# The norm of the sampled image channel by channel in one operation, and the last tap's copy on VectorE

## The chip, the cores and the metric

The kernel runs on one core of one Trainium2 chip. The metric is the device time of one execution in microseconds, as the median of several runs; lower is better. Before the change the three runs gave 17384.59, 17384.90 and 17401.33 us, median 17384.9.

## The reference, cut to what matters

A network of four layers works on `x` of shape (16, 32, 128, 128) in float32: 16 images, 32 channels, 128 x 128 pixels. Each layer adds its result to its input. The change lies in the last part of layer 1, a deformable convolution along a row of nine taps: each tap samples the normalised input at a row position that differs from pixel to pixel, then the nine samples are combined by a convolution, and a group norm over groups of four channels follows.

```python
K = 9
y = weight * yk + y_new
y_map = y.transpose(0, 2, 1, 3).reshape(Bn, Wd * K, Hd)
...
deformed = grid_sample_bilinear(input, grid)
out = conv2d(deformed, dsc_w, dsc_b, stride=(K, 1))
return group_norm(out, gn_w, gn_b, gn_w.shape[0] // 4)

# in the network
x = x + _L1_conv_ref(_gn(x), ...)
```

Before this part, other functions have made the sampling positions `y` for every tap and pixel (`ymap` in the kernel). A tap's column is a whole number, its row is not, so bilinear sampling is a weighted sum over rows, with the hat function max(0, 1 - |row - y|) as weight.

## The kernel before

The program runs through the layers one after the other. `layer1_sample` is the stage of the change. For each of the 16 images it holds the input as a tile `xt` of 128 rows (partitions) by 32 channels by 128 columns, and goes through 32 blocks of four columns. `order` lists all 512 (image, block) pairs; the loop variable `m` counts them, `n` is the block within its image, and `s, i = divmod(n, 4)` splits it into a group `s` of four blocks and the block's place `i` in the group.

**Sampling as a matmul.** For a tap the weights of all 128 rows are laid out as a hat matrix: row number against pixel. The kernel spreads the positions over all partitions, either with a DMA that broadcasts them (tile `yd`, taps 4 to 7, function `fetch`) or with matmuls by a selection matrix into PSUM tile `pb` (`spread`, tile `ya` for taps 0 to 3, tile `h8` for the ninth tap of a whole group of four blocks). ScalarE takes |y - row| of them (L1236 for `yd`, L1116 for `ya` and `h8`), VectorE makes min(., 1) - 1, the negative hat (`hats`, L1120). TensorE then multiplies `xt` by the hats (`sample`, L1127), 32 small matmuls per call, into a PSUM tile `pd` of 128 x 512; the pool of `pd` has two buffers. VectorE copies each `pd` to SBUF tile `ds` (L1274 for taps 0 to 3, L1280 for taps 4 to 7).

**The ninth tap.** Once a group, at `i == 3`, `last_tap` samples with `h8` into a `pd`, and that is copied to SBUF tile `ds8` (L1301), by ScalarE in this version. Straight after it VectorE makes the hats of the next group's `h8`.

**The convolution and the finish.** At `i == 0` of the next group `convolve` multiplies the group's samples by the weights (L1162, L1167) into PSUM tile `po`, and ScalarE adds the bias and copies (L1170). At `i == 1` `turn` transposes the result and VectorE copies it into the image's result tile `ob` (L1180), 128 partitions by 32 channels by 128. When an image's last group has been turned, `finish` starts for it. It is a Python generator: each `next(done)` at the end of a block of the next image issues its instructions up to the following `yield`. It has 22 such parts, so it spreads over blocks 1 to 22 of the next image: eight with the statistics of four channels each (L1193, L1194), two with small operations for mean and scale (two small matmuls by `avg`, L1197 and L1206), and twelve that apply the norm. The norm of four channels is a scale and an offset for each partition and channel, `sc` and `bi`, 128 x 8 x 4 each. The twelve parts are four slices `o` of eight channels with three operations of 128 x 1024 elements each: times `sc` (L1223), plus `bi` (L1225), both read by a broadcast along the 128 columns, and plus `xt` (L1227), after which GpSimd issues the DMA that stores the eight channels to `x2` (L1228). After the loop the rest of the last image's finish is issued at once.

**What sets the order.** TensorE, VectorE and ScalarE take their instructions in the order in which the program writes them, because the loop stands in `in_order`. GpSimd only stores the results here. The SP queue loads `yd` for every block (L1105), and per image `Y` and `Y8` (L1085, L1089) and `xt` in four pieces (L1093); their place on SP is chosen by the framework that schedules the program. `xt` has two buffers, so that its next load waits for the last L1227 of the image that used the buffer.

Of the kernel before, what the change touches and what calls it, by code (L numbers as in the profile page):

```python
# [12 lines left out]
ALU = mybir.AluOpType  # L13
# [4 lines left out]
P = 128  # L18
B, T, HW = 16, 32, 128
# [18 lines left out]
def rstd_of(nc, pool, var, n, m, tag):  # L38

    r = pool.tile([n, m], F32, name=tag, tag=tag)  # L40
    nc.vector.tensor_scalar_add(r, var, EPS)
    nc.scalar.activation(r, r, AF.Sqrt)
    nc.vector.reciprocal(r, r)
    return r


@contextmanager
def in_order(tc, *engines):

    traced = tc.nc.cur_bb.bb.instructions  # L50
    last = traced[-1]
    yield
    start = next(k for k in reversed(range(len(traced))) if traced[k] is last) + 1
    of = {e.engine: None for e in engines}
    for i in traced[start:]:
        if i.engine in of:
            if of[i.engine] is not None:
                tc.add_manual_dep(
                    i, of[i.engine].name,
                    mybir.DependencyInfo(mybir.DependencyClass.NoSync, mybir.DependencyReason.DATA),  # L60
                    reason="program order",
                )
            of[i.engine] = i
# [961 lines left out]
def layer1_sample(tc, w, x1, x2, ymap, sb1, batches=range(B)):  # L1025
# [9 lines left out]
    V, S, M = nc.vector, nc.scalar, nc.tensor.matmul  # L1035
# [3 lines left out]
    with ExitStack() as ctx:  # L1039
# [61 lines left out]
        def fetch(m):  # L1101
            b, n = order[m]
            blocks[m] = bl = {}
            bl["yd"] = yd = hp.tile([P, 4, W4], F32, name="yd", tag="yd", bufs=4)
            nc.sync.dma_start(  # L1105
                yd, ym(b)[4:8, n * W4 : n * W4 + W4].unsqueeze(0).to_broadcast([P, 4, W4])
            )
# [10 lines left out]
        def hats(t):  # L1118

            V.tensor_scalar(t, t, 1.0, 1.0, ALU.min, ALU.subtract)  # L1120
# [11 lines left out]
        def taps(m, k0, h):  # L1132
            b, n = order[m]
            pd = psd.tile([P, 4, HW], F32, name="pd", tag="pd")
            sample(
                pd, b,
                [
                    (q, i, 4 * n + i + k0 + q - 4, h[:, q, HW * i : HW * i + HW])
                    for i in range(4) for q in range(4)
                ],  # L1140
            )
            return pd
# [42 lines left out]
        def finish(b):  # L1185

            g, j = divmod(b, 4)
            im = images[b]
            ob, xt = im["ob"], im["xt"]
            st = sp.tile([P, 8, 6], F32, name="st", tag="st")  # L1190
            mv = sp.tile([P, 8, 2], F32, name="mv", tag="mv")
            for og in range(8):
                V.bn_stats(st[:, og], ob[:, 4 * og : 4 * og + 4])  # L1193
                V.bn_aggr(mv[:, og], st[:, og])  # L1194
                yield
            pm = pso.tile([P, 4, P], F32, name="pm", tag="pt")[:, 0, 0:8]
            M(pm, avg, mv[:, :, 0], start=True, stop=True)  # L1197
            mean = sp.tile([P, 8], F32, name="mean", tag="mean")
            V.tensor_copy(mean, pm)
            d = sp.tile([P, 8], F32, name="d", tag="d")  # L1200
            V.tensor_sub(d, mv[:, :, 0], mean)
            V.tensor_mul(d, d, d)
            V.tensor_add(d, d, mv[:, :, 1])
            yield
            pv = pso.tile([P, 4, P], F32, name="pv", tag="pt")[:, 0, 0:8]
            M(pv, avg, d, start=True, stop=True)  # L1206
            r = rstd_of(nc, sp, pv, P, 8, "r8")
            sc = sp.tile([P, 8, 4], F32, name="sc", tag="sc")
            V.tensor_mul(
                sc, rows[:, 0].rearrange("p (a b) -> p a b", b=4),  # L1210
                r.unsqueeze(2).to_broadcast([P, 8, 4]),
            )
            bi = sp.tile([P, 8, 4], F32, name="bi", tag="bi")
            V.tensor_mul(bi, sc, mean.unsqueeze(2).to_broadcast([P, 8, 4]))
            V.tensor_sub(bi, rows[:, 1].rearrange("p (a b) -> p a b", b=4), bi)
            yield
            for q in range(4):
                o = slice(8 * q, 8 * q + 8)
                col = [
                    t.rearrange("p a b -> p (a b)")[:, o].unsqueeze(2).to_broadcast([P, 8, HW])  # L1220
                    for t in (sc, bi)
                ]
                V.tensor_mul(ob[:, o], ob[:, o], col[0])  # L1223
                yield
                V.tensor_add(ob[:, o], ob[:, o], col[1])  # L1225
                yield
                V.tensor_add(ob[:, o], ob[:, o], xt[:, o])  # L1227
                nc.gpsimd.dma_start(  # L1228
                    x2[g][T * j + 8 * q : T * j + 8 * q + 8].rearrange("o (r c) -> r o c", c=HW),
                    ob[:, o],  # L1230
                )
                yield

        def absolutes(m):
            yd = blocks[m]["yd"]
            S.activation(yd, yd, AF.Abs, bias=nrow)  # L1236

        def near(m):
            b, n = order[m]
            blocks[m]["ya"] = ya = hp.tile([P, 4, W4], F32, name="ya", tag="ya")  # L1240
            spread(ya, images[b]["Y"], n, 32)

        def eighth(b, s):
            h8 = hp.tile([P, 4, W4], F32, name="h8", tag="h8", bufs=2)
            spread(h8, images[b]["Y8"], s, 8)
            images[b]["h8", s] = h8
# [5 lines left out]
        with in_order(tc, nc.tensor, nc.vector, nc.scalar):  # L1252
            eighth(batches[0], 0)
            near(0)
            absolutes(0)
            near(1)
            hats(images[batches[0]]["h8", 0])
            hats(blocks[0]["ya"])
            hats(blocks[0]["yd"])
            done = iter(())  # L1260
            for m in range(NM + 6):
                b, n = order[m] if m < NM else (None, m - NM)
                if m < NM:
                    bl = blocks[m]
                    bl["ds"] = dp.tile([P, 2, W4], F32, name="ds", tag="ds", bufs=6)
                    if n == 12 and m + NB < NM:
                        open_image(order[m + NB][0])
                    if m + 3 < NM:
                        fetch(m + 3)
                    pd = taps(m, 0, bl["ya"])  # L1270
                    if m + 1 < NM:
                        absolutes(m + 1)
                        hats(blocks[m + 1]["ya"])
                    V.tensor_copy(bl["ds"][:, 0], pd.rearrange("p i r -> p (i r)"))  # L1274
                    if m + 2 < NM:
                        near(m + 2)
                    pd = taps(m, 4, bl["yd"])
                    if m + 1 < NM:
                        hats(blocks[m + 1]["yd"])
                    V.tensor_copy(bl["ds"][:, 1], pd.rearrange("p i r -> p (i r)"))  # L1280
                s, i = divmod(n, 4)
                if i == 0 and 4 <= m <= NM:
                    bb, nn = order[m - 4]
                    ss = nn // 4
                    oc = convolve(
                        bb, ss, [blocks.pop(mm)["ds"] for mm in range(m - 4, m)],
                        images[bb].pop("ds8"),
                    )
                elif i == 1 and 5 <= m <= NM + 1:
                    turn(bb, ss, oc)  # L1290
                    if ss == NB // 4 - 1:
                        for _ in done:
                            pass
                        done = finish(bb)
                elif i == 2 and m + 2 < NM:
                    nb_, nn = order[m + 2]
                    eighth(nb_, nn // 4)
                elif i == 3 and m < NM:
                    pd = last_tap(b, s, images[b].pop(("h8", s)))
                    ds8 = dp.tile([P, W4], F32, name="ds8", tag="ds8")  # L1300
                    S.copy(ds8, pd.rearrange("p i r -> p (i r)"))  # L1301
                    images[b]["ds8"] = ds8
                    if m + 1 < NM:
                        nb_, nn = order[m + 1]
                        hats(images[nb_]["h8", nn // 4])
                next(done, None)
            for _ in done:
                pass
# [1033 lines left out]
```

## Time and profile before

The profiled execution took 17350.9 us, of which its span, from the first to the last instruction of the core, is 17349.1 us. The sampling stage lies between 11.17 and 14.36 ms of the span; ahead of it come layer 0 and the positions, behind it layers 2 and 3.

| | us |
|---|---|
| median of three runs | 17384.9 |
| profiled execution | 17350.9 |
| its span | 17349.1 |
| first load of positions into the stage to its last store | about 3190 |

The span's busy times by stretch (GpSimd is nearly idle in the sampling stage):

| stretch, ms | TensorE | VectorE | ScalarE | GpSimd | granted clock of TensorE |
|---|---|---|---|---|---|
| 0 to 5.7 | 5268 | 5380 | 4593 | 5628 | 0.99 |
| 6.5 to 11.9 | 4731 | 4992 | 3972 | 3786 | 0.94 |
| 11.9 to 17.35 | 4699 | 3891 | 3228 | 121 | 0.86 |

Within the sampling stage the start of the bias operation L1170, once per group of four blocks, is a clock tick. The mean interval between two of them, by the group's place in its image, is this (group 0 is blocks 1 to 4 in the image's numbering, group 1 is blocks 5 to 8, and so on, since L1170 runs in the first block of a group):

| group in the image | 0 | 1 | 2 | 3 | 4 | 5 | 6 | 7 |
|---|---|---|---|---|---|---|---|---|
| mean interval, us | 23.37 | 23.83 | 25.67 | 24.27 | 24.02 | 23.56 | 26.11 | 23.94 |
| parts of `finish` in it | 4 statistics | 4 statistics | mean, scale, 2 norm | 4 norm | 4 norm | 2 norm | none | none |

To read such tables: an engine's busy time counts every moment in which it has an instruction under way. On VectorE and ScalarE an instruction's own duration is longer than the distance to the next start, since the next begins before the last has drained; so a row's mean duration times its count overstates what an instruction takes of the engine. Distances between starts are named as such below.

### The profile page before, as it was taken

To read this page: it belongs to the slowest core of one execution; us is meant where nothing else is said; L and a number is where in the kernel's file an instruction comes from. 1 tells how busy PE (TensorE), PEld (TensorE's weight loads), DVE (VectorE), ACT (ScalarE), POOL (GpSimd) and SP (SyncE) were. 2 spreads that over 40 slices of the span, in tenths; PEclk is the share of its full clock that TensorE was granted. 3 is DMA by queue.
4 is the path that set the end of the run, shared out by engine and by line. 5 is a ranking of instruction groups with operands and counts; after the bars stand their busy time and mean duration, and the time that the engine had idled before them with its cause. 6 is when DMAs were issued, how large, how long until landed. Compare 5 with 4: busy or idle time off the path is not lost. (4 is left out here: it accounts for less than half of the span.)

```text
span 17349.1 us, 299637 instructions
## 1 busy us (share of the span) xinstructions
PE 15374.5 (89%) x113040; PEld 5889.8 (34%) x113040; DVE 14782.1 (85%) x14857; ACT 12219.8 (70%) x23708; POOL 9818.0 (57%) x18465
## 2 busy tenths in 40 slices
PE   8999999999999888888888888899999997688988
PEld 3333333333333322222222222255555552233433
DVE  9999999999999759999999999888888886777523
ACT  7888888888888647777777777698898882455311
POOL 9999999999999617778888888600000000000000
PEclk9999999999999989999999999898999888778888
DMA  0000000000000484444554445577777779444345
GB/s 22 12 12 12 12 12 16 12 12 12 12 13 10 70 146 155 164 161 156 166 163 163 164 161 167 158 187 198 198 196 194 198 196 206 89 77 79 72 117 177
DMA packets 1525970, 1884.46 MB, mean 109 GB/s; under 512 B 148837, under 2 KB 868765, under 8 KB 1513702
## 3 DMA queue, kind: packets, MB, share of 16 engines
q1 hardware_dynamic: 1413414, 1688.04, 37.6%
q10 hardware_dynamic: 84480, 83.91, 1.6%
q0 software_dynamic: 26624, 93.35, 1.5%
q8 instruction: 888, 14.55, 0.3%
q14 instruction: 564, 4.62, 0.1%
HBM read 1561.58 MB, written 229.64 MB: 103 GB/s over the span
## 5 line engine op out<-in xcount | busy, mean ns | idle before, releaser
L235 POOL TENSOR_SCALAR Rp<-su,nv 128x128 f32<-128x128 f32 x16384 | 5837.5, 378 | 71.7 <-PE pS L241 37.8
L224 DVE TENSOR_TENSOR Rd<-pu,nv 128x2048 f32<-128x2048 f32 x2176 | 4880.8, 2277 | 75.3 <-PE pS L241 71.6
L239 ACT ACTIVATE Ra<-su,bv 128x128 f32<-128x128 f32 x14336 | 4285.5, 388 | 540.9 <-PE pS L241 536.3
L241 PE MATMUL pS<-Rd,zw 128*32 128x512 f32 x17408 | 2907.3, 603 | 219.4 <-DVE Rd L224 219.1
L822 DVE TENSOR_TENSOR_SCAN hh<-dd,state,pd 128x512 f32<-128x512 f32 x2304 | 2823.0, 1267 | 153.7 <-PE py L856 10.6
L843 POOL TENSOR_TENSOR hh<-hh,bc 128x2048 f32<-128x2048 f32 x512 | 2319.8, 4531 | 458.4 <-DVE state L830 455.2
L241 PE MATMUL pS<-Rp,zw 128*32 128x512 f32 x8192 | 2012.3, 596 | 175.1 <-POOL Rp L235 173.2
L807 PE MATMUL pd<-du,spread 32*128 32x512 f32 x4608 | 1352.1, 661 | 571.0 <-DVE hh L822 563.1
L1228 POOL DMA_DIRECT2D x<-ob x64 | 89.4, 1396 | 3098.8 <-DVE ob L1227 2762.4
L799 ACT ACTIVATE dd<-dd,m_a 128x512 f32<-128x512 f32 x2304 | 1515.2, 714 | 339.0 <-DMA dd<-dm 328.2
L817 DVE TENSOR_TENSOR pd<-pd,bc 128x1024 f32<-128x1024 f32 x1152 | 1400.5, 1216 | 61.8 <-ACT bc L780 53.0
L241 PE MATMUL pS<-Ra,zw 128*32 128x512 f32 x7168 | 1276.2, 600 | 0.0
L1236 ACT ACTIVATE yd<-yd,nrow 128x2048 f32<-128x2048 f32 x512 | 1235.2, 2412 | 39.9 <-DMA yd<-ymap 39.9
L1116 ACT ACTIVATE ya<-pb,nrow 128x1024 f32<-128x1024 f32 x1024 | 1191.3, 1255 | 81.8 <-PE pb L1115 81.6
L1115 PE MATMUL pb<-Y,sel 32*128 32x512 f32 (+1 forms) x5120 | 1089.2, 744 | 160.6 <-ACT ya L1116 157.4
L241 PEld LDWEIGHTS pS<-Rd,zw 128*32 128x32 f32 x17408 | 623.7, 109 | 1225.2 <-issue 586.8
L807 PEld LDWEIGHTS pd<-du,spread 32*128 32x128 f32 x4608 | 373.7, 191 | 1611.6 <-DVE hh L822 717.7
L241 PEld LDWEIGHTS pS<-Rp,zw 128*32 128x32 f32 x8192 | 443.2, 109 | 1322.6 <-POOL Rp L235 863.3
L1120 DVE TENSOR_SCALAR yd<-yd 128x2048 f32<-128x2048 f32 x512 | 724.4, 1415 | 184.6 <-ACT yd L1236 183.4
L1120 DVE TENSOR_SCALAR ya<-ya 128x2048 f32<-128x2048 f32 x512 | 753.8, 1472 | 9.9 <-ACT ya L1116 8.8
L1127 PE MATMUL pd<-ya,xt 128*32 128x128 f32 x16384 | 688.7, 310 | 40.6 <-DVE ds L1280 29.6
L1127 PEld LDWEIGHTS pd<-yd,xt 128*32 128x32 f32 x16384 | 539.8, 178 | 470.2 <-issue 232.9
(421 smaller groups left out, 23716.8 us busy)
## 6 DMA issues: line engine op xcount, KB each, us to landing
dd<-dm SPq DMA_DIRECT2D x2304, 256.0 KB
yd<-ymap SPq DMA_DIRECT2D x512, 1024.0 KB
hw<-x SPq DMA_DIRECT2D x192, 512.0 KB
dm<-dt POOLq DMA_DIRECT2D x192, 256.0 KB, 3.9
xb<-tok SPq DMA_DIRECT2D x248, 144.0 KB
w<-d SPq DMA_DIRECT2D x64, 528.1 KB
x<-in_x SPq DMA_DIRECT2D x64, 512.0 KB
x<-o SPq DMA_DIRECT2D x128, 256.0 KB
```

What stands on the lines that cost most here:

```text
L224: nc.vector.tensor_tensor(R, st["pu"].unsqueeze(1).to_broadcast([P, 4, 4, HW]), nv[:, :, i::32].rearrange("p t q -> p q t").unsqueeze(3).t ...
L235: nc.gpsimd.tensor_scalar(R[:, q, k], su[:, k], 3.4028234e38, nv[:, k, c], ALU.min, ALU.max)
L239: nc.scalar.activation(R[:, q, k], su[:, k], AF.Relu, bias=bv[:, k, c])
L241: nc.tensor.matmul(st["pS"][32 * q : 32 * q + 32], zw[:, 31 - i : 63 - i], R[:, q], start=first, stop=False, tile_position=(0, 32 * q), sk ...
L799: S.activation(dd[:, r], dd[:, r], AF.Exp, scale=acol[:, dr, d : d + 1])
L807: nc.tensor.matmul(pd[:, a], spread[e, k], st["du"][n][e], start=True, stop=True)
L817: V.tensor_mul(pd, pd, bm.unsqueeze(1).to_broadcast([P, 2, CH]))
L822: V.tensor_tensor_scan(hh[:, r, s], dd[:, r, s], pd[:, a, s], st["state"][:, 4 * i + r : 4 * i + r + 1], ALU.mult, ALU.add,)
L843: G.tensor_mul(hh, hh, st["bc"][1, n].unsqueeze(1).to_broadcast([P, 4, CH]))
L1120: V.tensor_scalar(t, t, 1.0, 1.0, ALU.min, ALU.subtract)
L1127: M(pd[32 * q : 32 * q + 32, i], xt[:, :, xc], h, start=True, stop=True, tile_position=(0, 32 * q),)
L1236: S.activation(yd, yd, AF.Abs, bias=nrow)
```

## The change

Two edits, both in `layer1_sample`. In `finish`, the two operations over eight channels with broadcast scale and offset are replaced by eight operations of one channel each, which multiply and add in one instruction, with the scale and the offset of that channel as scalars per partition. There is a `yield` after every fourth channel, so a slice still takes two parts for these and one for the addition of `xt`. In the loop, the copy of the last tap's samples from PSUM to `ds8` is issued on VectorE instead of ScalarE.

```diff
+            scf, bif = (t.rearrange("p a b -> p (a b)") for t in (sc, bi))
             yield
             for q in range(4):
                 o = slice(8 * q, 8 * q + 8)
-                col = [
-                    t.rearrange("p a b -> p (a b)")[:, o].unsqueeze(2).to_broadcast([P, 8, HW])
-                    for t in (sc, bi)
-                ]
-                V.tensor_mul(ob[:, o], ob[:, o], col[0])
-                yield
-                V.tensor_add(ob[:, o], ob[:, o], col[1])
-                yield
+                for c in range(8 * q, 8 * q + 8):
+                    V.tensor_scalar(
+                        ob[:, c], ob[:, c], scf[:, c : c + 1], bif[:, c : c + 1], ALU.mult, ALU.add
+                    )
+                    if c % 4 == 3:
+                        yield
                 V.tensor_add(ob[:, o], ob[:, o], xt[:, o])
...
                     ds8 = dp.tile([P, W4], F32, name="ds8", tag="ds8")
-                    S.copy(ds8, pd.rearrange("p i r -> p (i r)"))
+                    V.tensor_copy(ds8, pd.rearrange("p i r -> p (i r)"))
                     images[b]["ds8"] = ds8
```

## The prediction

> **What bounds the kernel now.** I read the page first, then the busy time by stretch, then, inside the sampling stage, groups by line, waits, the chain of waits and the order of time.
>
> ```profile
> span 17349.1 us, 299637 instructions
> 11200.00:14340.00 3140.00, 2892.62 (x44842) 1701.46 (x44838) 2725.17 (x2903) 2795.74 (x2060) 85.81 (x60) 0.90 0.76 195
> ```
>
> The second line is the sampling stage: its length, then busy time of TensorE matmuls, weight loads, VectorE, ScalarE and GpSimd, then the granted clock. TensorE is busy 92%, ScalarE 89%, VectorE 87%: three engines in lock step, none of them plainly the bound. The diff touches only this stage, so everything is decided in these 3140 us, which are 128 groups of four blocks at 24.4 us each.
>
> ```profile
> L1280 DVE COPY ds<-pd 128x512 f32<-128x512 f32 x459 | 341.1, 743 | 50.9 <-PE pd L1127 50.2
> L1120 DVE TENSOR_SCALAR h<-h 128x2048 f32<-128x2048 f32 x115 | 197.3, 1715 | 0.0
> L1301 ACT COPY ds<-pd 128x512 f32<-128x512 f32 x115 | 102.2, 889 | 30.7 <-PE pd L1127 30.2
> L1225 DVE TENSOR_TENSOR ob<-ob,bi 128x1024 f32<-128x1024 f32 x59 | 86.1, 1459 | 0.0
> L1223 DVE TENSOR_TENSOR ob<-ob,sc 128x1024 f32<-128x1024 f32 x58 | 84.7, 1460 | 0.0
> ```
>
> These are the rows the change touches or that price it (window 11500 to 14300). L1223 and L1225 go; L1301 moves from ScalarE to VectorE, where L1280 is the same copy of the same shape from the same PSUM tile.
>
> ```profile
> PEld pb L1115 <- ACT ya L1116: 282.6, 321, 4.8
> ACT oc L1170 <- PE po L1167: 107.2, 124, 1.7
> ACT ds L1301 <- PE pd L1127: 38.1, 41, 5.1
> ```
>
> Who waited for whom (total us, times, longest). TensorE does wait for ScalarE, but for the spread rows ya, in block 2 of a group, where ScalarE also makes h. The second line matters most: right after the block that holds the copy, ScalarE waits for the convolution in 124 groups, 0.87 us each. Time that the copy gives back runs into that wait.
>
> ```profile
> 12624.54 1.72 PE pd L1127 x30
> 12626.26 0.02 issue
> 12626.28 0.69 DVE ds L1280
> 12626.98 1.59 DVE h L1120
> 12628.57 0.60 DVE st L1193
> ...
> 12638.23 0.61 DVE ob L1180
> 12638.83 0.04 issue
> 12638.88 0.39 PE pm L1197 x2
> ```
>
> The chain of waits (start, length, what) of one image. In block 7 it comes from TensorE's taps, goes into VectorE's copy, then into the hats of h, and stays on VectorE for 12 us, until TensorE's mean matmul can start. The new copy goes between the second and third instruction of this run. Going through the chain over the whole stage: VectorE's h directly behind L1280 lies on it in 32 of 128 groups, 13 of these in block 7 of an image; L1223 and L1225 lie on it with 42.5 of their 161 us in the loop (26%); ScalarE's L1301 is never on it.
>
> **How much of VectorE's work reaches the time.** The kernel holds its own experiment: the finish of the image before is spread over blocks 1 to 22 of an image, so groups carry different VectorE loads. Intervals between starts of L1170, means over the images: groups 0 and 1 (four statistics of 0.95 us each, 3.8 us) 23.37 and 23.83; group 5 (two norm operations, 2.7 us) 23.56; groups 3 and 4 (four, 5.4 us) 24.27 and 24.02. So 3.43 us of such work give 23.59 us and 5.38 us give 24.15: 0.56/1.95 = 0.28 us of time per us of VectorE work, outside the places where the chain already runs through it. Group 7, with no such work, takes 23.94, so the share may also be near 0; I keep 0 and 1 as ends.
>
> **The change part by part.**
>
> *Copy of ds8 onto VectorE.* One per group. Start to next start L1280 takes 0.60 us (median). It also waits for the last tap's matmuls, which TensorE does after those that L1280 waits for: the record has their end 0.2 us behind the start of h in most groups, 28 us in all, mean 0.22. So 0.82 us per group, 105 us on VectorE. Behind the copy stand the hats of h, the finish's operation, the hats of ya and the next ds copy; TensorE waits for the last of these when it wants the PSUM buffer. Where the chain runs there, the whole counts: 32 x 0.83 = 27 us. In the other 96 groups the cover is TensorE's convolution in block 0 (L1162 and L1167, 1.72 + 1.07 us in the chain): 96 x 0.82 x 0.28 = 22 us, ends 0 and 79.
>
> *Copy off ScalarE.* Frees 128 x 0.72 us (start to next start) and 39 us of waiting, 132 us. I take 0: the chain never has it, and the wait for po swallows it. Ends 0 and -132.
>
> *Norm.* 64 pairs of 1024-element operations become 64 x 8 operations of 128 elements with two scalars read from SBUF. Removed, start to next start: 1.340 + 1.336 = 2.68 us. The new form is not in the trace; the neighbours are:
>
> ```profile
> 21.83 5.25 DVE L175 TENSOR_SCALAR x<-x,cols 128x256 f32<-128x256 f32 x16
> ...
> 12263.56 0.23 DVE L1097 TENSOR_SCALAR w<-dsc_k,cb 128x64 f32<-128x64 f32 x1
> 12263.71 0.33 DVE L1099 TENSOR_SCALAR w<-dsc_k,cb 128x128 f32<-128x128 f32 x1
> 12263.94 1.22 DVE L1120 TENSOR_SCALAR ya<-ya 128x2048 f32<-128x2048 f32 x1
> ```
>
> L175 has the same two scalars in place on 256 elements: 5.17 us for 16 starts (the next instruction starts at 27.00), 0.32 each. L1099 has 128 elements and one scalar from SBUF: 0.20 (mean of its pitches). L203, 128 elements and no scalar read, 0.13. From L1097 to L1099 64 more elements lengthen the minimum by 38 ns, so 128 fewer than L175 save 0.08: I take 0.25, between ends 0.13 and 0.32. Eight: 2.0 us (1.04 to 2.56), so a pair saves 0.66 (0.12 to 1.64). In the loop 60 pairs x 0.66 x 0.28 = -11 us (0 to -28 at that share, -98 if all counted). The yields stay twelve per image, so nothing moves to another block. The last image is finished after the loop, VectorE alone on the path (starts 14343.86, 14345.12, 14346.38, so 2.52 per pair): 4 x 0.5 = -2 us (0 to -6). The stores are the same.
>
> [...]
>
> **Sum.** 27 + 22 + 0 - 11 - 2 = +36 us. The profiled execution took 17350.9 (span 17349.1 and 1.8 around it), so 17387 in its terms. The median of the three runs, 17384.9, is 34 us above it; there the forecast is 17421, slower by 0.21%. A measurement of this kernel can tell about 0.2%, 35 us, from no change: 17350 to 17420 is "within".
>
> **Rivals.**
> 1. *Hidden.* The convolution covers the copy wherever the chain does not run through h: 27 - 11 - 2 = +14, 17399, within 0.2%. For it: group 7's time. Against it: 88 of 127 groups would make VectorE wait for the last tap, and VectorE idles only 13% of the stage.
> 2. *ScalarE is the bound, and is relieved* (the other side). In block 2 TensorE stands still for ScalarE about once a group (282.6 us over 321 waits). If ScalarE enters that block earlier, groups shrink by up to 1.03 us. Where it does, VectorE's lateness is hidden, so at a share s of the groups the change is 49(1-s) - 132s - 13: below nothing from s = 20%, by over 0.2% from 39%, and at a half -55, 17330. Against it: the wait for po lies between the copy and block 2, and 0.87 us of wait merely becomes 1.9.
> 3. *Clock.* Groups cluster at 23.1 and 24.5 us, and stretches of the stage run at half clock (stage mean 0.90). If later copies make TensorE pause once more in half of the groups, 64 x 1.4 = +90: 17475. Against it: most new waits are 0.2 us.
> 4. *SP's order.* Only TensorE, VectorE and ScalarE have a fixed order; yd and the next image's xt are both loaded by SP, and the xt loads wait for the last L1227. Group 6, where yd comes late, takes 26.11 against 23.59, 2.5 us in 15 images. A shifted order doubles or removes that: 38 us on top of the hidden case's 14, either way: 17437 or 17361.
>
> That the change doesn't do what it says I exclude: both edits are plain in the code.
>
> **Chances.** Forecast 0.37 (17421; as much of it below 17420 as its bounds allow is counted under "within", 0.07), hidden 0.22, ScalarE relieved 0.22, clock 0.11, SP 0.08 (half each; its better half ends within). Faster: 0.22. Slower: 0.30 + 0.11 + 0.04 = 0.45. Within: 0.07 + 0.22 + 0.04 = 0.33. Range: from the relief in a bit under half of the groups, 17335, to the clock case in most of its size, 17465; the forecast's own range is 17400 to 17455 (copy off the chain at a share of 0.1 to 0.6, norm at 0 to -18).
>
> **What would show it.** VectorE's last-tap copies at about 0.74 us each, waiting for TensorE in more than half of the groups; 512 operations at L1223 or near with starts 0.25 apart; ScalarE's wait for po up from 107 us to over 200; intervals of groups 0, 1 and 7 longer by 0.2 to 0.8, those of 3 and 4 hardly changed. Wrong if the wait for po stays and TensorE's wait for ya shrinks (rival 2), or if group 6 alone moves (rival 4).

## The result, and the profile after

The changed kernel takes 17416.88 us as the median of 12 runs (17355.43 to 17453.24). The kernel before, run beside it, takes 17396.46 (12 runs with the three of before, 17359.32 to 17443.78). The ratio is 1.0005 with a 95% interval of 0.9992 to 1.0019: no change that can be told from none. The forecast, slower by 0.21%, lies just above that interval; the rival "hidden" at +14 us lies inside it.

Both kernels scatter by half a per cent from run to run. Cutting each profiled execution at the first and the last start of L1170 and at the end of the last addition of `xt` shows where (us):

| kernel | ahead of first L1170 | first to last L1170 | to end of last addition | behind |
|---|---|---|---|---|
| before | 11238.6 | 3093.1 | 26.78 | 2990.5 |
| before_again | 11234.2 | 3086.8 | 26.77 | 2979.8 |
| after | 11267.2 | 3098.6 | 25.67 | 2977.2 |
| after_again | 11270.3 | 3101.4 | 25.69 | 2976.2 |
| copy_only | 11240.6 | 3085.8 | 26.76 | 2973.4 |
| copy_only_again | 11300.2 | 3094.3 | 26.78 | 2976.3 |
| norm_only | 11184.9 | 3090.6 | 25.68 | 2983.4 |

What lies ahead of the stage, which the change leaves alone, varies by 115 us over these executions (they ran on several chips); the stage itself varies by under 10 us for one kernel. So the second column is the measure from here on, and the profiled execution of after, 19.6 us longer in its span than that of before, owes 28.6 us to the part ahead of the stage, 5.5 to the stage, -1.1 to the tail and -13.3 to what comes after.

The page's first line of after, and the stretch of the stage (columns as before: length, TensorE, weight loads, VectorE, ScalarE, GpSimd, clock):

```profile
span 17368.7 us, 300066 instructions
11200.00:14340.00 3140.00, 2857.24 (x44456) 1678.48 (x44454) 2726.79 (x3359) 2705.74 (x1925) 84.32 (x60) 0.91 0.77 196
```

VectorE's busy time did not rise (2725 before, 2727 now), ScalarE's fell by 90 us, and the time stayed. The rows of the touched operations in the window 11500 to 14300 (busy us, mean ns, then idle time before them):

```profile
L1279 DVE COPY ds<-pd 128x512 f32<-128x512 f32 x457 | 345.1, 755 | 61.2 <-PE pd L1127 61.0
L1221 DVE TENSOR_SCALAR ob<-ob,sc,bi 128x128 f32<-128x128 f32 x472 | 153.5, 425 | 0.0
L1120 DVE TENSOR_SCALAR h<-h 128x2048 f32<-128x2048 f32 x115 | 146.9, 1277 | 0.0
L1300 DVE COPY ds<-pd 128x512 f32<-128x512 f32 x115 | 114.9, 999 | 17.2 <-PE pd L1127 16.8
```

Two things were not foreseen. The copy takes 999 ns on VectorE, where its twin L1279 takes 755. And the hats of h, which the change doesn't touch, fell from 1715 to 1277 ns. In the order of time (start, length), before:

```profile
12260.02 0.68 DVE L1280 COPY ds<-pd 128x512 f32<-128x512 f32 x1
12260.62 1.57 DVE L1120 TENSOR_SCALAR h<-h 128x2048 f32<-128x2048 f32 x1
12262.12 1.53 DVE L1223 TENSOR_TENSOR ob<-ob,sc 128x1024 f32<-128x1024 f32 x1
```

and after, at the same place of the image and in a later block:

```profile
12285.10 0.67 DVE L1279 COPY ds<-pd 128x512 f32<-128x512 f32 x1
12285.70 1.09 DVE L1300 COPY ds<-pd 128x512 f32<-128x512 f32 x1
12286.72 1.20 DVE L1120 TENSOR_SCALAR h<-h 128x2048 f32<-128x2048 f32 x1
12287.84 1.42 DVE L1221 TENSOR_SCALAR ob<-ob,sc,bi 128x128 f32<-128x128 f32 x4
...
12304.44 1.11 DVE L1221 TENSOR_SCALAR ob<-ob,sc,bi 128x128 f32<-128x128 f32 x4
12305.46 1.23 DVE L1120 TENSOR_SCALAR ya<-ya 128x2048 f32<-128x2048 f32 x1
```

What stands right behind L1280 (L1279 in after) is slow in both kernels: h before, with a mean of 1715 ns, and the copy now, with 999. And a run of four small operations takes 1.35 us at one time and 1.02 at another, start to next start (rows overlap: L1280 above lasts 0.68 us, and h starts 0.60 behind its start). The waits of after:

```profile
PEld pb L1115 <- ACT ya L1116: 271.0, 308, 4.5
ACT oc L1170 <- PE po L1167: 186.5, 124, 2.3
DVE ds L1300 <- PE pd L1127: 18.1, 72, 1.0
```

ScalarE's wait for po took up most of the freed time, 107 to 187 us; the forecast was over 200. TensorE's wait for ya hardly changed (282.6 before, 271.0 now).

### The profile page after: what moved, and what is told of

Read it like the earlier page. It is cut to its first block, busy times and chain, and to the rows that moved or that the text cites. A ratio compares the mean times of both kernels' runs of the same rounds, so it can differ in the third digit from the quotient of the medians.

```text
span 17368.7 us, 300066 instructions
## 1 busy us (share of the span) xinstructions
PE 15285.6 (88%) x113040; PEld 5829.6 (34%) x113040; DVE 14928.3 (86%) x15369; ACT 12138.9 (70%) x23580; POOL 9782.3 (56%) x18465
## 5 line engine op out<-in xcount | busy, mean ns | idle before, releaser
L241 PE MATMUL pS<-Rd,zw 128*32 128x512 f32 x17408 | 2872.4, 605 | 346.6 <-DVE Rd L224 344.5
L822 DVE TENSOR_TENSOR_SCAN hh<-dd,state,pd 128x512 f32<-128x512 f32 x2304 | 2824.0, 1267 | 152.7 <-PE py L856 13.3
L241 PE MATMUL pS<-Rp,zw 128*32 128x512 f32 x8192 | 1890.0, 596 | 129.9 <-POOL Rp L235 126.1
```

The source lines that it names most:

```text
L241: nc.tensor.matmul(st["pS"][32 * q : 32 * q + 32], zw[:, 31 - i : 63 - i], R[:, q], start=first, stop=False, tile_position=(0, 32 * q), sk ...
L822: V.tensor_tensor_scan(hh[:, r, s], dd[:, r, s], pd[:, a, s], st["state"][:, 4 * i + r : 4 * i + r + 1], ALU.mult, ALU.add,)
```

## The experiments

**Each part alone, and the scatter.** `copy_only` has the second hunk of the diff, `norm_only` the first; the other two are the unchanged kernels.

```diff
-                    S.copy(ds8, pd.rearrange("p i r -> p (i r)"))
+                    V.tensor_copy(ds8, pd.rearrange("p i r -> p (i r)"))
```

> The last tap's copy on VectorE, the norm as before. Measure: time from the first to the last start of L1170 (127 groups; 3093.1 us before, 3098.6 after the change) beside the whole time. The prediction's terms: 27 + 22 = +49 us, so 3142 us and +0.28% in time. Theory of a moved slowdown: the hats of h overlap the next taps on TensorE in every group and take 1.61 us start to next start there; with the copy ahead of them they fall to about 1.18 and the copy itself takes 0.89, so VectorE gains only 0.89 + 0.14 of waiting - 0.43 = 0.6 us per group; at a share of 0.28 that is +21 us: 3114. Theory of hidden work (rival 1, all covered outside the chain): at most +19 us, 3112, and as little as 0.

> The norm channel by channel, the copy on ScalarE as before. The prediction's terms: -11 us in the loop and -2 behind it: 3082 us from first to last L1170, tail from the last L1170 to the end of the last addition 26.8 - 2 = 24.8. From the trace of after: four small operations take 1.17 us start to next start against 1.34 of one large, so 120 x 0.17 = 20 us less on VectorE, at a share of 0.28 -6 us: 3087; tail 25.7.

> The changed kernel once more, for the scatter of the stage from one execution to the next. If the stage is steady: first to last L1170 within 10 us of 3098.6 while the whole time may differ by tens of us. If the scatter of the whole time lies in this stage: as far off as the whole time is.

> The kernel before once more, for the same. Steady stage: within 10 us of 3093.1. Otherwise as far off as the whole time is.

Measured: ratio 1.0006 (0.9993 to 1.0019) for the copy alone and 0.9995 (0.9982 to 1.0008) for the norm alone. The stage takes 3085.8 us with the copy and 3090.6 with the norm, against 3093.1 and 3086.8 before: neither part moves it. For the stage as a whole the copy's +49 us of the prediction are out, and so are the 21 of the smaller price. The stage is steady to 6 us in the two runs of each whole kernel (to 9 in the two of `copy_only`), while the whole time isn't.

**Is the copy covered, or paid and repaid by ScalarE?** Both explain a zero. Four kernels, each with extra work that nobody reads, profiled once each:

```diff
# both_copies (two_scalar: the same with S.copy)
                     S.copy(ds8, pd.rearrange("p i r -> p (i r)"))
+                    ds9 = dp.tile([P, W4], F32, name="ds9", tag="ds9")
+                    V.tensor_copy(ds9, pd.rearrange("p i r -> p (i r)"))
# two_vector
-                    S.copy(ds8, pd.rearrange("p i r -> p (i r)"))
+                    V.tensor_copy(ds8, pd.rearrange("p i r -> p (i r)"))
+                    ds9 = dp.tile([P, W4], F32, name="ds9", tag="ds9")
+                    V.tensor_copy(ds9, pd.rearrange("p i r -> p (i r)"))
# copy_sload
-                    S.copy(ds8, pd.rearrange("p i r -> p (i r)"))
+                    V.tensor_copy(ds8, pd.rearrange("p i r -> p (i r)"))
+                    ds9 = dp.tile([P, W4], F32, name="ds9", tag="ds9")
+                    S.copy(ds9, bl["ds"][:, 0])
```

> The kernel before with the last tap copied twice: by ScalarE as before, and by VectorE into a tile that nobody reads. VectorE's new load without ScalarE's relief. First to last L1170 (before: 3093.1 and 3086.8; copy on VectorE alone: 3085.8). Theory 'covered' (VectorE's copy costs nothing because its lateness is made good in the convolution's block): 3085 to 3096. Theory 'paid and repaid' (it costs some 20 us, and ScalarE's relief gives them back): 3105 to 3115. The prediction's price for the copy: 3139.

> The kernel before with the last tap copied twice by ScalarE, the second into a tile that nobody reads: the relief with its sign turned. 'Covered', with the wait for po as ScalarE's cover: 3085 to 3096, and ScalarE's wait for po falls from 107 to below 60 us. 'Paid and repaid': 3105 to 3115.

> The copy on VectorE and then once more on VectorE, into a tile that nobody reads; none on ScalarE. VectorE's load doubled at the same place. 'Covered' with slack left: 3085 to 3100. 'Covered', slack used up by the first copy: each further 0.6 us shows, 128 x 0.6 = 77 us at the most, 3105 to 3170. The prediction's share: 2 x 49 us, 3188.

> The last tap's copy on VectorE, and in its old place on ScalarE a copy of the same size from an SBUF tile (the block's first ds) into a tile that nobody reads: VectorE's load of the change without ScalarE's relief, and without both engines at the same PSUM tile, which in both_copies made VectorE wait 115 us for ScalarE. First to last L1170: 'covered': 3085 to 3098. 'Paid and repaid' by ScalarE's relief: 3105 to 3115.

> The copy on VectorE alone once more. If the 10 us between the kernel before (3093.1, 3086.8) and the changed one (3098.6, 3101.4) come from the copy and 3085.8 was a lucky run: 3096 to 3102. If the copy costs nothing: 3084 to 3094.

| kernel | first to last L1170, us |
|---|---|
| before, twice | 3093.1, 3086.8 |
| copy_only, twice | 3085.8, 3094.3 |
| copy_sload | 3090.3 |
| two_scalar | 3095.5 |
| both_copies | 3118.3 |
| two_vector | 3120.9 |

The first of these to be run, `both_copies`, spoke for "paid and repaid": +28 us. But its waits show that it did something else as well:

```profile
DVE ds L1303 <- ACT ds L1301: 115.1, 95, 2.3
PEld pd L1127 <- DVE ds L1303: 61.4, 80, 0.9
```

VectorE stood still for 115 us until ScalarE's copy of the same PSUM tile was done, and TensorE then waited for the late buffer. So it lengthened VectorE's stretch by more than one copy, and says nothing about the relief. (Whether the chip or the order given by the program holds two engines apart on one PSUM tile was not tried.) `copy_sload` gives ScalarE a copy of the same length back from another tile (899 ns), and the stage stays at 3090.3, so ScalarE's relief doesn't pay for the copy. (Its wait for po is 137.7 us there, 107.2 in before and 189.5 in `copy_only`: most of the relief is gone, not all.) `two_scalar` turns the relief's sign: ScalarE has a further copy, and the stage is at 3095.5, within the scatter of the measure. The waits of `copy_sload`, then of `two_scalar`:

```profile
ACT oc L1170 <- PE po L1167: 137.7, 124, 1.7
ACT oc L1170 <- PE po L1167: 51.3, 100, 1.6
```

107 us of waiting became 51 with the second copy on ScalarE; that wait is ScalarE's cushion in both directions. And `two_vector` shows that more load does reach the time: a second copy costs 31 us over the mean of the two runs of `copy_only` (3090.1). It takes 0.60 us itself, start to next start, but h goes from 1.17 back to 1.50 behind it, so the stretch from the first ds copy to the instruction behind h grows from 2.90 to 3.81 us: 116 us over the stage, of which 0.27 show.

"Covered" is true of the sum alone. Split by place, with the time in which TensorE's granted clock was at half (added up from the clock records of the traces):

| kernel | mean interval of group 2, us | the other 111 intervals, us | half clock in the stage, us |
|---|---|---|---|
| before, twice | 25.67, 25.69 | 2682.4, 2675.8 | 584, 563 |
| norm_only | 25.57 | 2681.5 | 573 |
| two_scalar | 26.10 | 2677.9 | 543 |
| copy_only, twice | 26.05, 26.55 | 2668.9, 2669.6 | 519, 515 |
| copy_sload | 26.41 | 2667.8 | 509 |
| after, twice | 26.88, 26.27 | 2668.4, 2681.0 | 543, 591 |
| both_copies | 27.30 | 2681.6 | 550 |
| two_vector | 27.07 | 2687.8 | 526 |

With the copy alone on VectorE (three runs) the 16 intervals of group 2 are 0.69 us longer than in before and norm_only, 11 us in all, and the other 111 together are 11 us shorter. The shorter part goes with less time at half clock, 514 us against 573. Among the intervals of one place, a microsecond more at half clock goes with 0.20 to 0.33 us more length in these eleven traces, 0.26 over all; so 59 us less are an estimated 15 us. Why the clock was at half for less time is open: `after_again` has the copy too, and 591 us. No run holds the clock equal.

**What makes the place behind L1280 slow?** Sorting the VectorE operations of before by what TensorE did meanwhile: the hats yd and ya take 1.23 us where no tap matmul ran beside them (165 and 70 cases) and 1.59 to 1.61 where tap matmuls ran for more than 0.8 us of it (167 and 224); every h had them (107 cases), at 1.72. ScalarE's L1236 behaves alike: 2.02 us (28 cases) against 2.48 (364). The tap matmuls differ from the others in their weights, 32 elements of `xt` that lie 128 elements apart. `packed` takes 32 neighbours instead; it samples other values than the reference, and serves for timing alone:

```diff
-                    pd[32 * q : 32 * q + 32, i], xt[:, :, xc], h,
+                    pd[32 * q : 32 * q + 32, i], xt[:, xc // 4, 32 * (xc % 4) : 32 * (xc % 4) + 32], h,
```

> The kernel before, but each tap's weights are 32 neighbouring elements of xt instead of 32 elements 128 apart; so it samples other values, and the output is not the reference's; counts and shapes of all instructions stay. Theory of the moved slowdown: VectorE's hats take 1.23 us with no tap matmuls beside them and 1.59 to 1.72 with them because these read their weights with a stride; then all hats fall to about 1.2, h to 1.2, and VectorE's load falls by some 200 us. If the matmuls' other operand or PSUM is the cause: 1.6 and more stay. The stage: if VectorE's load is covered and nothing else changes, 3080 to 3095; if the weight loads of 179 ns fall to the 110 ns of L1162's, which are packed, TensorE gains up to 128 x 9 x 32 x 69 ns = 2544 us of load time, most of it under its matmuls, and the stage may fall below 3000.

Groups of before and then of `packed`, window 11300 to 13900:

```profile
L1236 ACT ACTIVATE yd<-yd,nrow 128x2048 f32<-128x2048 f32 x426 | 1029.7, 2417 | 26.8 <-DMA yd<-ymap 26.8
L1127 PEld LDWEIGHTS pd<-ya,xt 128*32 128x32 f32 x13660 | 462.3, 179 | 252.4 <-DVE ds L1280 107.4 <-issue 48.0 <-DVE yd L1120 44.9
L1120 DVE TENSOR_SCALAR h<-h 128x2048 f32<-128x2048 f32 x107 | 183.6, 1716 | 0.0
L1301 ACT COPY ds<-pd 128x512 f32<-128x512 f32 x107 | 97.4, 910 | 26.9 <-PE pd L1127 26.4
```

```profile
L1236 ACT ACTIVATE yd<-yd,nrow 128x2048 f32<-128x2048 f32 x464 | 928.4, 2001 | 68.5 <-DMA yd<-ymap 68.5
L1127 PEld LDWEIGHTS pd<-ya,xt 128*32 128x32 f32 x14818 | 413.2, 117 | 260.0 <-DVE ds L1280 112.7 <-issue 58.1 <-DVE ya L1120 36.2
L1120 DVE TENSOR_SCALAR h<-h 128x2048 f32<-128x2048 f32 x116 | 141.1, 1217 | 0.0
L1301 ACT COPY ds<-pd 128x512 f32<-128x512 f32 x116 | 68.3, 589 | 22.1 <-PE pd L1127 21.5
```

More blocks fit into the same 2600 us (464 for 426), h is at 1217 ns, ScalarE's L1236 at 2001, its copy at 589 instead of 910, the weight loads at 117 instead of 179. The stage fell from 3093 to 2843.5 us. The hats beside tap matmuls now take as long as those without, 1.22 us both. So in this stage the stride of the weight loads lengthens the loads themselves (179 against 117 ns for ya) and, while they run, operations of VectorE (h 1716 against 1217) and of ScalarE (L1236 2417 against 2001). How the 250 us divide between TensorE's loads and the two other engines was not separated. The stage was also at half clock for 488 us instead of 584, by the price above an estimated 25 of the 250.

**A version that beats both.** `packed_real` computes the reference's result with packed weights: `xt` is held as columns x channels.

```diff
-            im["xt"] = xt = xp.tile([P, T, HW], F32, name="xt", tag="xt")
+            im["xt"] = xt = xp.tile([P, HW, T], F32, name="xt", tag="xt")
...
             for q in range(4):
-                nc.sync.dma_start(xt[:, 8 * q : 8 * q + 8], xg[:, 8 * q : 8 * q + 8])
+                o = slice(8 * q, 8 * q + 8)
+                xq = xp.tile([P, 8, HW], F32, name="xq", tag="xq", bufs=2)
+                (nc.sync if b == batches[0] else nc.gpsimd).dma_start(xq, xg[:, o])
+                nc.gpsimd.tensor_copy(xt[:, :, o].rearrange("p c o -> p o c"), xq)
...
-                    pd[32 * q : 32 * q + 32, i], xt[:, :, xc], h,
+                    pd[32 * q : 32 * q + 32, i], xt[:, xc], h,
...
-                V.tensor_add(ob[:, o], ob[:, o], xt[:, o])
+                V.tensor_add(ob[:, o], ob[:, o], xt[:, :, o].rearrange("p c o -> p o c"))
```

> The kernel before with xt held as columns x channels, so that a tap's weights are 32 neighbouring elements: quarters of the image come into a small tile (by SP for the first image, by GpSimd's queue for the others), and GpSimd, idle in this stage, writes them in the other order; the addition of xt reads with a stride. If the stride of the weight loads is what slows VectorE and ScalarE, the stage keeps most of the 250 us that the run with packed weights won: first to last L1170 2840 to 2920, time 0.985 to 0.991 of before. If GpSimd's strided writes or the strided addition bring the slowdown back: above 3000.

> The same with both parts of the change. If the change is free because VectorE's load is covered, it is free here too, where VectorE has more room: within 10 us of packed_real. If the moved slowdown is what made the copy on VectorE cheap before (h got shorter by 0.43 us), the copy now costs its full 0.6 us, at a share of 0.28 +21 us at most.

Measured: `packed_real` 17129.14 us against 17381.42 beside it, ratio 0.9863 (0.9839 to 0.9887), stage 2807.8; with both parts of the change, `packed_after`, 0.9857 (0.9837 to 0.9878), stage 2801.6. What the new layout costs stands in the groups of `packed_real`:

```profile
L1096 POOL COPY xt<-xq 128x1024 f32<-128x1024 f32 x55 | 143.4, 2650 | 280.0 <-PE pd L1130 125.0 <-DMA xq<-x 86.7 <-PE pb L1118 41.0
L1283 DVE COPY ds<-pd 128x512 f32<-128x512 f32 x468 | 321.0, 686 | 52.7 <-PE pd L1130 51.9
L1123 DVE TENSOR_SCALAR h<-h 128x2048 f32<-128x2048 f32 x117 | 158.4, 1354 | 0.0
L1230 DVE TENSOR_TENSOR ob<-ob,xt 128x1024 f32<-128x1024 f32 x56 | 111.5, 1990 | 0.0
L1304 ACT COPY ds<-pd 128x512 f32<-128x512 f32 x117 | 68.8, 588 | 28.4 <-PE pd L1130 27.9
```

GpSimd had room (busy for 75 of the 2600 us in before), but its four copies of 2.65 us per image are not without effect; the addition with the strided operand takes 1.99 us, where the one with neighbouring elements took 1.46 in before and 1.21 in `packed`. That h is at 1.35, between 1.22 and 1.72, goes with GpSimd's copies: 104 of the 117 take 1.22 us, and the 13 that such a copy overlaps take 2.44. Shortest, median and longest, in ns:

```profile
L1123 DVE TENSOR_SCALAR h<-h x117: 1209/1217/2455, 11311.3 to 13886.3; 128x2048 f32<-128x2048 f32 x117
```

Nor is the gain that of the packing alone. The loads of `xt` went from SP's queue, where they stood beside those of `yd`, to GpSimd's: group 6, in which ScalarE waits up to 7.7 us for `yd` in `packed`, takes 27.28 us there and 21.66 here, while other groups are longer by up to 1.5. The new queue without the packing was not tried. The change costs nothing here either: 2801.6 and 2807.8 lie as close as two runs of one kernel.

## Why the prediction was right in its range and wrong in its size

**The whole time: luck.** 17416.88 us is 4 us from the forecast's 17421, but the kernel before ran at 17396.46 beside it, 12 us above the three runs that the forecast started from, and the difference of the two can't be told from none.

**The norm's new operation: right in kind, short by a tenth or more.** The price was 0.25 us start to next start, 2.0 for eight, from the quickest rows of its kind: L175 has 0.32 in the sixteen starts that were read, and 0.37 as the mean of its 256. Undisturbed the new operation takes 0.255 (four in 1.02 us above). In the tail eight take 2.17 us up to the addition:

```profile
14377.99 2.13 DVE L1221 TENSOR_SCALAR ob<-ob,sc,bi 128x128 f32<-128x128 f32 x8
14380.16 1.22 DVE L1226 TENSOR_TENSOR ob<-ob,xt 128x1024 f32<-128x1024 f32 x1
```

and 2.22 in the other three slices; the tail shrank by 1.1 us, where 2 were forecast. In the loop the mean over the 120 runs of four is 1.14 us (1.17 in `norm_only`), so eight take 2.28 to 2.33 and a pair saves 0.35 to 0.40, not 0.66. Of the forecast -11 us nothing can be seen: 3090.6.

**The copy's load on VectorE: 0.82 us forecast, 0.68 found.** From the start of the ds copy ahead of h to the instruction behind h it took 2.22 and 2.20 us in two runs of before, 2.87 to 2.93 in the five runs that have the one copy on VectorE and no second one of the same tile. The parts are others than forecast: the copy takes 0.89 and not 0.60, and now stands beside the tap matmuls (they run for 0.92 of its mean duration of 0.99 us in after); h takes 1.18 instead of 1.61, and less of it does (0.41 us, 1.34 before). The wait for the last tap was right: from the start of the ds copy to the start of the new one it takes 0.81 to 0.84 us (0.92 in `after_again`) instead of 0.61, so 0.2 to 0.3 where 0.22 was forecast. (The 18 us in 72 cases above count only the time in which VectorE stood idle.)

**The share of VectorE's load that reaches the time: this step failed for the stage, and held in one place.** It was taken as the whole in the 32 groups where the chain runs through h (27 us) and 0.28 elsewhere (22 us). Over the stage the runs show 0 for this load, +0.68 us in every group, and ScalarE's relief is not what pays for it. But block 7, where 13 of the 32 lay, did what was forecast: its chain ends in block 9, in group 2, which grew by 11 us with the copy alone; 13 x 0.83 = 11 us were to be had there. The other 38 us were not seen: the 111 other intervals became shorter by 11 us, together with the time at half clock. Whether the load outside block 7 is covered or was paid for by the clock is open. The 0.28 came from comparing groups with different parts of `finish`; these differ also in where the work stands in the group and in the disturbances of groups 2 and 6, and three points are a thin line. The second copy shows about that share of what it adds (0.27), the first none: the share isn't one number.

**ScalarE's relief: 0, as far as the runs can tell,** and for the reason given: its wait for po grew to 187 us, and with a second copy shrank to 51.

**The intervals that were to show it.** Groups 0, 1 and 7 were to grow by 0.2 to 0.8 us; they moved by +0.12, -0.02 and -0.34. Groups 3 and 4 were to stay: -0.06 and -0.68. The sign was looked for in the wrong place: it stands in group 2, where after has 26.88 and 26.27 in its two runs against 25.67 and 25.69. Together the two parts have 3098.6 and 3101.4 us where before has 3093.1 and 3086.8 and each part alone stays at the lower level on average. Those 10 us, 0.06% of the time, are little more than the up to 8.5 us by which one kernel's runs differ; whether they belong to the two parts together was not settled. The two runs of after also have more time at half clock (543 and 591 us) than the three with the copy alone (509 to 519).

**The rows of the copy.** The prediction expected VectorE's copy at about 0.74 us, the row of L1280 in before (743 ns, where ScalarE's L1301 had 889); it took 999. In `packed` the two rows of the kernel before are 684 and 589, in `packed_real` 686 (L1283) and 588 (L1304): the order turns, and both rows of before held the slowdown measured beside the strided weight loads.

## What to carry to other kernels

A sum of zero can be a cost at one place and a gain at others: compare place by place, with the granted clock beside it, before you call a load covered. A dummy load of the same size is a cheap test, but read in its trace what it really added. When an untouched instruction gets faster after an edit, ask what ran beside its old place: here that question led to a version that is 1.4% faster, where the edit itself brought nothing. Compare the stage and not the whole time when the scatter comes from code that the change doesn't touch.

## What the hardware showed that was not expected

The taps' weight loads of 128 x 32 float32 took 179 (ya) and 178 ns (yd) in before, where the 32 elements of a partition lie 512 bytes apart, and 117 and 115 in `packed`, where they are neighbours; those of h took 140 and 113. Beside the strided ones, VectorE's hats of 2048 elements took 1.59 to 1.72 us instead of 1.23 in before, and ScalarE's L1236 2.48 instead of 2.02; ScalarE's copy out of PSUM took 910 ns there and 589 in `packed`, without them. The hats of h that one of GpSimd's copies overlaps took 2.44 us instead of 1.22 (13 cases in `packed_real`). What VectorE and ScalarE wait for in these operations no run here shows.
